# Attention kernel on one core: rows of a batch placed as 16j+f, so that a head-split tile moves in one transfer instead of four

## The chip, the cores and the metric

The kernel runs on one core of one Trainium2 chip. The metric is the device time of one execution in microseconds. Three runs of the kernel before gave 780.52, 779.7 and 776.21 us, median 779.7.

## The reference

The input x is 8 batches of 512 rows by 512 columns in float32. Each batch has a condition vector that is projected too and added to the queries and keys; 16 heads of 32 columns attend over all 512 rows, and the result is added to x.

```python
Q = _split_heads(x @ Wq.T + bq)
K = _split_heads(x @ Wk.T + bk)
V = _split_heads(x @ Wv.T + bv)
cQ = Q + _split_heads(tokens @ Wq.T + bq)
cK = K + _split_heads(tokens @ Wk.T + bk)
scores = jnp.einsum('bhqd,bhkd->bhqk', cQ, cK) / jnp.sqrt(jnp.float32(HEAD_DIM))
attn = jax.nn.softmax(scores, axis=-1)
out = jnp.einsum('bhqk,bhkd->bhqd', attn, V)
return x + out.transpose(0, 2, 1, 3).reshape(B, S, D_MODEL)
```

Nothing in it depends on the order of the 512 rows, as long as the same order is used for queries, keys, values, residual and output of a batch.

## The kernel before, in words

The work is cut into 32 items t = 4b + g: batch b, and a group g of four heads, that is 128 columns. Weights and inputs stand transposed in SBUF (features on the partitions); the projections are made by a scheme with seven products of half-size blocks instead of eight (`product`, L459, `item`). For each item the scores are computed by rows (L642), their maxima are taken on VectorE (L615), and exponentials with row sums on ScalarE (L690).

Three of the four row blocks of an item's exponentials are not computed again in transposed form but "kept": VectorE turns 32x32 blocks in place (`turn_kept`, L661), and then two block rows have to change places between partitions. That is `swap_kept` (L678): block 0 goes to a side buffer (move 0), block 1 to the place of block 0 (move 1), the side buffer to the place of block 1 (move 2). Each move is two transfers within SBUF, for the first two row blocks (part 0, 256 KB each, 32 partitions of 8 KB) and for the third (part 1, 128 KB each). Each move waits until the move ahead has landed. For the last row block the scores are computed again in transposed form (L772, L782); its exponentials (L792) and the kept ones are multiplied with V (L820, L837). L837 also reads a copy of V with its partition halves exchanged, which `cross_v` (L813) makes once per batch in two halves of two transfers.

All of these transfers stand in one queue, that of SP (SyncE), in the order in which the code is written: SP issues one after the other, and where one has to wait for data or for a landing, all behind it wait too. `step(t)` is a round of the loop. In a round SP issues: part 0's moves 0 and 1, a small transposing transfer of maxima (`turn_max`, L725), part 0's move 2, part 1's move 0, the output of item t-1 (`put`, L908), in the first round of each batch half of `cross_v`, part 1's moves 1 and 2, a chunk of the next batch's x (`load_block`, L167), the residual of item t+1 (`load_residual`, L185), and in the second round of a batch the other half of `cross_v`. L837 of item t-1, in round t, needs all moves of round t-1.

A chunk of x, a residual and an output have the same form: a tile of 128 partitions with 16 x 32 values each. Partition 32h+j, place f holds the 32 columns of head h of the group in row 32f+j of the batch. DRAM holds the rows of 512 columns, so such a tile is 2048 pieces of 32 values, 128 bytes each. In one access pattern over DRAM, partition 32h+j would be stepped by two strides (h by 32 values, j by a row), and f by a third (32 rows). The kernel issues one transfer for each h, whose pattern is `spread(a, d)`, j outermost (32), then f (16), then 32 values.

Item 30's output is made at the end in one tile and stored by `store_30` (L1377), two of the four transfers by SP and two by ACT; item 31's output is untransposed by TensorE and stored by two transfers (L1416). The first batch's x is loaded by `load_x` (L152) in four chunks of 128 rows of 2 KB.

Of the kernel before, what the change touches and what calls it, by code (L numbers as in the profile page):

```python
# [17 lines left out]
def kernel(  # L18
# [38 lines left out]
    nc = tc.nc  # L57
    P = 128
    B, S, D = x.shape
    HD = 32  # L60
    H = D // HD
    G = D // P
    HG = P // HD
    NP = HG // 2
    NS = S // P
# [66 lines left out]
    def take(n):  # L132
        got = [order.pop(0) for _ in range(n)]
        return got

    def give(*bs):
        order.extend(bs)
# [8 lines left out]
    xs = {}  # L146

    def load_x(n, queue=nc.sync):

        if n < B * NS:  # L150
            xs[n] = early[:, 3 + n, :]
            queue.dma_start(xs[n], x[n // NS, n % NS * P : (n % NS + 1) * P, :])  # L152

    BL = 32
    NB = S // BL

    def spread(a, d):

        return a.rearrange("(f j) d -> j f d", j=BL)[:, :, d : d + BL]

    def load_block(n):

        b, cc = divmod(n, NC)
        if b < B:
            xs[n] = xp.tile([P, NB, BL], F32, tag="x", name=f"x_{n}")
            for h in range(HG):
                nc.sync.dma_start(xs[n][h * BL : (h + 1) * BL], spread(x[b], cc * P + h * BL))  # L167

    xr = {}
    late = []  # L170

    def turned_by_vector(t):

        return t < T - 1

    def load_residual(t):

        b, g = divmod(t, G)
        if turned_by_vector(t):
            if t == T - 2:  # L180
                xr[t] = late[0][:, 2, :].rearrange("p (f e) -> p f e", e=BL)
            else:
                xr[t] = op.tile([P, NB, BL], F32, tag="xr", name=f"xr_{t}")
            for h in range(HG):
                nc.sync.dma_start(  # L185
                    xr[t][h * BL : (h + 1) * BL], spread(x[b], g * P + h * BL)
                )
        else:

            xr[t] = xT[b][:, g, :]  # L190
# [187 lines left out]
    def combine_x(b, half, on=nc.vector):  # L378

        if b >= B:  # L380
            return
        blk = [[xT[b][:, i * 2 : i * 2 + 2, j * HS : (j + 1) * HS] for j in range(2)] for i in range(2)]
        to = [xc[:, i, :, :] for i in range(4)]
        if half == 0:
            on.tensor_tensor(to[2], blk[1][1], blk[0][1], ALU.subtract)
            on.tensor_tensor(to[1], to[2], blk[0][0], ALU.add)
        else:
            on.tensor_tensor(to[0], blk[0][1], blk[0][0], ALU.subtract)
            on.tensor_tensor(to[3], blk[1][0], to[1], ALU.subtract)
# [240 lines left out]
    def rows(t, qc, bs):  # L630

        open_max(t)
        for j in range(HG):
            row_scores(t, qc, j, psum[:, bs[j], :])
# [30 lines left out]
    def swap_kept(t, move, part):  # L665

        qs = slice(0, 2) if part == 0 else slice(2, KQ)
        w = (qs.stop - qs.start) * HG * HS
        for h in range(2):

            def block(a):
                e = kept[t][h * 64 + a * BL : h * 64 + (a + 1) * BL, 1 - a, qs]
                return e.rearrange("p q j x e -> p (q j x e)")

            at = (1 - h) * 64 + part * BL
            side = between[at : at + BL, :w]
            to, of = [(side, block(0)), (block(0), block(1)), (block(1), side)][move]
            nc.sync.dma_start(to, of)  # L678
# [178 lines left out]
    def masked(t):  # L857

        if t in aparts:
            return aparts.pop(t)  # L860
        apart = op.tile([P, HG, NS, NS], F32, tag="apart", name=f"apart_{t}")
        nc.gpsimd.tensor_tensor(  # L862
            apart,
            sums[t].rearrange("p c h o -> p h c o").broadcast_to([P, HG, NS, NS]),
            which.unsqueeze(1).unsqueeze(1).broadcast_to([P, HG, NS, NS]),
            ALU.mult,
        )
        return apart
# [11 lines left out]
    def reciprocals(t, pd):  # L880
        rec = op.tile([P, NB, 1], F32, tag="recs", name=f"recs_{t}")
        nc.vector.reciprocal(rec, psum[:, pd, :NB].unsqueeze(2))
        return rec
# [20 lines left out]

    def put(t, y):
        b, g = divmod(t, G)
        for h in range(HG):
            nc.sync.dma_start(spread(out[b], g * P + h * BL), y[h * BL : (h + 1) * BL])  # L908

    def untranspose(o, pt):  # L910
        for qc in range(NS):
# [201 lines left out]
    def third(t):  # L1113

        if t % G == 1 and t > 1:
            cross_v(t // G, 1)
        k3 = take(HG)
        rows(t, 2, k3)
        maxima(t, 2, k3)
        row_exponentials(t, 2, k3)  # L1120
        give(*k3)
        turn_kept(t, 1)
        swap_kept(t, 0, 0)
        swap_kept(t, 1, 0)

    def rest_and_sums(t):

        hi, pd = take(1)[0], take(1)[0]
        if t in KEPT:
            times_v_rest(t, hi)  # L1130
        else:
            for kc in range(NS):
                times_v(t, kc, psum[:, hi, :])
        spread_sums(masked(t), psum[:, pd, :])
        return hi, pd
# [5 lines left out]
    def step(t):  # L1141

        b, r = divmod(t, G)
        third(t)
        at = take(2)
        multiply, leave, sums_of = item(*next(made), at)
        multiply()
        hi, pd = rest_and_sums(t - 1)
        leave(0)
        leave(1)  # L1150
        rec = reciprocals(t - 1, pd)
        give(*at, pd)
        aparts[t] = masked(t)
        sums_of()
        if r == 0:
            combine_x(b + 1, 0, nc.gpsimd)

        n = take(HG)
        rows(t + 1, KQ, n)
        maxima(t + 1, KQ, n)  # L1160
        row_exponentials(t + 1, KQ, n)
        split_max(t + 1)
        turn_max(t + 1)
        if t - 1 in KEPT:
            lo = take(1)
            y = kept_leaves(t - 1, lo[0], hi)
        else:
            lo = []
            y = turned(t - 1, hi)
        give(*n[:3], *lo, hi, n[3])  # L1170
        swap_kept(t, 2, 0)
        finish(t - 1, y, rec)
        turn_kept(t, 2)
        if t == 1:
            turn_next()
        swap_kept(t, 0, 1)
        put(t - 1, y)
        if r == 0:
            cross_v(b, 0)

        s = take(HG)
        scores_of_rest(t, s)
        rest_leaves(s)
        give(*s)
        k1 = take(HG)
        rows(t + 1, 0, k1)
        maxima(t + 1, 0, k1)
        swap_kept(t, 1, 1)
        swap_kept(t, 2, 1)
        if t > 1:  # L1190
            bias_residual(t)
        at = take(2)
        multiply, leave, sums_of = item(*next(made), at)
        multiply()
        row_exponentials(t + 1, 0, k1, (0, 1))
        leave(0)
        row_exponentials(t + 1, 0, k1, (2, 3))
        leave(1)
        give(k1[0], k1[1], at[0], k1[2], k1[3], at[1])
        turn_next()  # L1200
        if r == 0:
            combine_x(b + 1, 1, nc.gpsimd)
        sums_of()

        k2 = take(HG)
        rows(t + 1, 1, k2)
        maxima(t + 1, 1, k2)
        row_exponentials(t + 1, 1, k2)
        give(*k2)
        turn_kept(t + 1, 0)  # L1210
        more = next(made, None)
        if more:
            at = take(2)
            multiply, leave, sums_of = item(*more, at)
            multiply()
            leave(0)
            leave(1)
            sums_of()
            give(*at)
        load_blocks()  # L1220
        load_residual(t + 1)

    for t in KEPT[:-1]:
        step(t)
# [51 lines left out]
    t = T - 3  # L1276
# [12 lines left out]
    n = more_maxima(t + 1, 0)  # L1289
    lo = take(1)[0]  # L1290
    y = kept_leaves(t - 1, lo, hi)
# [25 lines left out]
    y = kept_leaves(t, lo, hi)  # L1317
# [3 lines left out]
    n = more_maxima(t + 2, 0)  # L1321
# [6 lines left out]
    t = T - 2  # L1328
# [19 lines left out]
    t = T - 1  # L1348
# [19 lines left out]
    y30 = op.tile([P, NB, BL], F32, tag="res", name=f"res_{t - 1}")  # L1368
# [4 lines left out]

    def store_30(queue, hs):
        b, g = divmod(t - 1, G)
        for h in hs:
            queue.dma_start(spread(out[b], g * P + h * BL), y30[h * BL : (h + 1) * BL])  # L1377

    store_30(nc.sync, (0, 1))
    exponentials(t, 3, (4, 2, 0, 1))  # L1380
# [13 lines left out]
    y = late[0][:, 1, :].rearrange("p (c s) -> p c s", c=NS)  # L1394
    rec = op.tile([P, NS, HG, 1], F32, tag="rec", name="rec")
    pi, po = bank(6), [bank(4), bank(2)]
    b, g = divmod(t, G)
# [10 lines left out]
    for i in range(2):  # L1408
        cs = slice(i * 2, i * 2 + 2)
        nc.vector.tensor_tensor(  # L1410
            y[:, cs].rearrange("p c (h e) -> p c h e", h=HG),
            po[i][:, two[i]].rearrange("p (c h e) -> p c h e", c=2, h=HG),
            rec[:, cs].broadcast_to([P, 2, HG, HD]),
            ALU.mult,
        )
        (nc.scalar, nc.sync)[i].dma_start(  # L1416
            out[b].rearrange("(c p) d -> p c d", p=P)[:, cs, g * P : (g + 1) * P], y[:, cs]
        )


# [29 lines left out]
```

## Time and profile before

| | |
|---|---|
| median of three runs | 779.7 us (776.21 to 780.52) |
| the profiled execution | 782.4 us, of which the span on the core is 780.6 us |
| busy, share of the span | PE 88%, DVE 76%, ACT 65%, POOL 54% |
| granted clock of TensorE | 0.931 |
| DMA packets | 233595, of them 216554 under 512 B |

The profile lists a busy time for each engine, but SP appears in it only as a queue: its rows (SPq) are the times in which a transfer was being issued, waits included. A transfer's own time is told in two ways: the share of time in which the sixteen DMA engines moved packets, and the time from issue to landing. How much of the work of a queue matters is seen from the waits of the computing engines.

### The profile page before, as it was taken

Reading aid. Unit: us, or ns where it says so; the run is one execution under the profiler, and the core shown is the slowest. Engines: PE = TensorE matmul, PEld = TensorE weight load, DVE = VectorE, ACT = ScalarE, POOL = GpSimd, SP = SyncE. Lnnn points to the kernel's source line nnn. Section 1 sums busy time; section 2 is a strip of 40 time slices with the busy share of each in tenths; the row PEclk is TensorE's granted clock in tenths of the full one; section 3 lists DMA queues with packets and bytes.
Section 4 is the critical chain, followed back from the end, with each engine's and each line's share of the span. In section 5 each row is a group of like instructions: output and inputs, shape, how many; then the busy total and the mean of one; then the engine's idle time right before and its main releaser. Section 6 shows DMA issues by size and latency. Waiting matters only on the chain. (4 is left out here: it accounts for less than half of the span.)

```text
span 780.6 us, 29911 instructions
## 1 busy us (share of the span) xinstructions
PE 688.8 (88%) x12524; PEld 397.8 (51%) x12524; DVE 592.5 (76%) x913; ACT 510.8 (65%) x1310; POOL 418.3 (54%) x537
## 2 busy tenths in 40 slices
PE   9999989859989599896998769988799979997697
PEld 7444545535546355453555345554455546554352
DVE  3895997738896398883988839968498858888567
ACT  2584887638885287863877828858388848885145
POOL 2716474835657256673566716657266755653230
PEclk9999999979999799996999969989799979998789
DMA  6444677767666776776666677767767766767711
GB/s 172 76 72 96 132 156 155 152 150 139 142 144 143 155 146 137 154 163 150 136 136 143 158 159 145 152 138 148 166 136 151 157 151 141 151 140 161 170 25 28
DMA packets 233595, 107.86 MB, mean 138 GB/s; under 512 B 216554, under 2 KB 217066, under 8 KB 227892
## 3 DMA queue, kind: packets, MB, share of 16 engines
q1 hardware_dynamic: 231700, 104.90, 64.4%
q8 instruction: 98, 1.61, 0.9%
q10 hardware_dynamic: 1760, 1.05, 0.5%
q14 instruction: 37, 0.30, 0.1%
HBM read 19.75 MB, written 8.39 MB: 36 GB/s over the span
## 5 line engine op out<-in xcount | busy, mean ns | idle before, releaser
L615 DVE TENSOR_REDUCE nmax<-psum 128x1 f32<-128x512 f32 x498 | 305.5, 674 | 32.9 <-PE psum L642 32.7
L690 ACT ACTIVATE store<-psum,nmax 128x512 f32<-128x512 f32 x348 | 235.7, 692 | 41.1 <-DVE nmax L615 40.6
L661 DVE STREAM_TRANSPOSE store<-store 128x1024 f32<-128x1024 f32 x174 | 204.2, 1212 | 0.0
L642 PE MATMUL psum<-kT,qT 32*128 32x512 f32 x1024 | 164.9, 645 | 2.0 <-ACT store L690 1.5
L792 ACT ACTIVATE store<-psum 128x512 f32<-128x512 f32 x116 | 59.9, 604 | 137.6 <-PE psum L782 137.6
L837 PE MATMUL psum<-store,v 64*32 64x192 f32 x1856 | 69.0, 397 | 57.1 <-DMA store<-store 39.8
L894 DVE STREAM_TRANSPOSE res<-psum 128x192 f32<-128x192 f32 x58 | 18.9, 363 | 130.1 <-issue 111.5
L690 ACT ACTIVATE psum<-psum,nmax 128x512 f32<-128x512 f32 x132 | 87.1, 660 | 32.3 <-DVE nmax L615 31.6
L902 POOL TENSOR_TENSOR res<-res,recs 128x512 f32<-128x512 f32 x30 | 31.4, 1047 | 123.5 <-DVE res L895 120.9
L837 PEld LDWEIGHTS psum<-store,v 64*32 64x32 f32 x1856 | 44.5, 126 | 91.0 <-issue 39.8
L837 PE MATMUL psum<-store 64*32 64x192 f32 x1856 | 67.3, 388 | 24.3 <-DMA store<-v 23.4
L642 PEld LDWEIGHTS psum<-kT,qT 32*128 32x128 f32 x1024 | 54.7, 191 | 37.6 <-ACT store L690 19.5
L690 ACT ACTIVATION_READ_ACCUMULATOR store<-psum,nmax 128x1 f32 x348 | 72.9, 210 | 0.0
L837 PEld LDWEIGHTS psum<-store 64*32 64x32 f32 x1856 | 50.1, 127 | 31.5 <-DMA store<-v 27.2
L459 PE MATMUL psum<-wc_v,xc 128*32 128x256 f32 x768 | 47.7, 379 | 0.1
L198 POOL TENSOR_TENSOR xr<-xr,bvs 128x512 f32<-128x512 f32 x30 | 38.5, 1285 | 12.0 <-DMA x<-in_x_dram 8.5
L459 PE MATMUL psum<-xc,wc_q 128*32 128x256 f32 x720 | 44.5, 379 | 0.0
L459 PE MATMUL psum<-xc,wc_k 128*32 128x256 f32 x720 | 44.5, 379 | 0.0
L782 PEld LDWEIGHTS psum<-qT,kT 32*128 32x128 f32 x928 | 38.2, 220 | 4.3 <-issue 3.3
L903 POOL TENSOR_TENSOR res<-res,xr 128x512 f32<-128x512 f32 x30 | 38.5, 1284 | 2.4
L782 PE MATMUL psum<-qT,kT 32*128 32x128 f32 x928 | 38.4, 307 | 0.9 <-issue 0.8
L862 POOL TENSOR_TENSOR apart<-sums,which 128x64 f32<-128x64 f32 x30 | 8.8, 292 | 53.9 <-ACT store L690 53.9
(207 smaller groups left out, 1109.9 us busy)
## 6 DMA issues: line engine op xcount, KB each, us to landing
store<-store SPq DMA_DIRECT2D x174, 256.0 KB, 3.4
store<-store SPq DMA_DIRECT2D x174, 128.0 KB, 3.0
store<-v SPq DMA_DIRECT2D x32, 256.0 KB, 3.8
out_dram<-res SPq DMA_DIRECT2D x122, 64.0 KB, 2.8
xr<-in_x_dram SPq DMA_DIRECT2D x120, 64.0 KB, 2.8
x<-in_x_dram SPq DMA_DIRECT2D x112, 64.0 KB, 2.5
w_q<-in_L_cond_Wq_dram SPq DMA_DIRECT2D x4, 256.0 KB, 3.8
w_v<-in_L_cond_Wv_dram SPq DMA_DIRECT2D x16, 64.0 KB, 2.4
```

Source lines behind the costliest of these rows:

```text
L198: nc.gpsimd.tensor_tensor(xr[t], xr[t], bias, ALU.add)
L459: nc.tensor.matmul(pt[r], still[:, r], moving, start=(kc == kcs[0]), stop=(kc == kcs[-1]))
L615: nc.vector.tensor_reduce(nmax[t][:, qc, j : j + 1, 0], pt, AX.X, ALU.max, negate=True)
L642: nc.tensor.matmul(pt, qkT["q", t][r, qc * P : (qc + 1) * P], qkT["k", t][r, :], start=True, stop=True,)
L661: nc.vector.transpose(e, e)
L690: nc.scalar.activation(to, of, AF.Exp, bias=nmax[t][:, qc, j, :], accum_out=sums[t][:, qc, j, :],)
L782: nc.tensor.matmul(psum[:, bs[j], kc * P : (kc + 1) * P], qkT["k", t][r, kc * P : (kc + 1) * P], qkT["q", t][r, R:], start=False, stop=(kc ...
L792: nc.scalar.activation(rest_of[:, j], psum[:, bs[j], :], AF.Exp)
L837: nc.tensor.matmul(psum[j * HD : (j + 1) * HD, (lo, hi)[h], : R // 2], v[half, c, (g * HG + j) * HD : (g * HG + j + 1) * HD], kept[t][half ...
L894: nc.vector.transpose(to[:, h], of.rearrange("p (c s) -> p c s", c=KQ))
L902: nc.gpsimd.tensor_tensor(y, y, rec.broadcast_to([P, NB, BL]), ALU.mult)
L903: nc.gpsimd.tensor_tensor(y, y, xr.pop(t), ALU.add)
```

## The change

Position 32f+j of a batch now holds row 16j+f instead of row 32f+j. With that, j and f step through the rows of a batch in one piece (row 16j+f), and the DRAM side of a whole tile can be written as one pattern with three steps: h outermost (4 steps of 32 values), then the 512 rows, then 32 values. A chunk of x, a residual and an output each become one transfer of 256 KB. `blocks(a, c)` is that pattern.

The other places follow: `load_x` reads rows 16j+f for four values of f at a time (DRAM pattern: f outermost with 4, then j with 32, then 512 values). `store_30` stores two heads by one transfer of 128 KB. The last item's output goes out by four transfers of 64 KB instead of two of 128 KB, two from each queue. And one line of `step` is moved: part 0's move 2 stands behind part 1's move 0, instead of ahead of it. The condition, biases and weights are loaded as before.

```diff
-            queue.dma_start(xs[n], x[n // NS, n % NS * P : (n % NS + 1) * P, :])
+            at = n % NS * HG
+            queue.dma_start(xs[n], x[n // NS].rearrange("(j f) d -> f j d", f=S // HD)[at : at + HG])
...
+    def blocks(a, c):
+
+        return a.rearrange("(j f) (c h e) -> c h j f e", f=NB, h=HG, e=BL)[c]
...
-            for h in range(HG):
-                nc.sync.dma_start(xs[n][h * BL : (h + 1) * BL], spread(x[b], cc * P + h * BL))
+            nc.sync.dma_start(xs[n].rearrange("p f e -> p (f e)"), blocks(x[b], cc))
...
-            for h in range(HG):
-                nc.sync.dma_start(
-                    xr[t][h * BL : (h + 1) * BL], spread(x[b], g * P + h * BL)
-                )
+            nc.sync.dma_start(xr[t].rearrange("p f e -> p (f e)"), blocks(x[b], g))
...
-        for h in range(HG):
-            nc.sync.dma_start(spread(out[b], g * P + h * BL), y[h * BL : (h + 1) * BL])
+        nc.sync.dma_start(blocks(out[b], g), y.rearrange("p f e -> p (f e)"))
...
-        swap_kept(t, 2, 0)
         finish(t - 1, y, rec)
         turn_kept(t, 2)
         if t == 1:
             turn_next()
         swap_kept(t, 0, 1)
+        swap_kept(t, 2, 0)
         put(t - 1, y)
...
-        for h in hs:
-            queue.dma_start(spread(out[b], g * P + h * BL), y30[h * BL : (h + 1) * BL])
+        of = y30[hs[0] * BL : (hs[-1] + 1) * BL].rearrange("p f e -> p (f e)")
+        queue.dma_start(blocks(out[b], g)[hs[0] : hs[-1] + 1], of)
...
-        (nc.scalar, nc.sync)[i].dma_start(
-            out[b].rearrange("(c p) d -> p c d", p=P)[:, cs, g * P : (g + 1) * P], y[:, cs]
-        )
+        rows_of = out[b].rearrange("(j c a) d -> c a j d", c=NS, a=HG)
+        for c in (i * 2, i * 2 + 1):
+            (nc.scalar, nc.sync)[i].dma_start(rows_of[c][:, :, g * P : (g + 1) * P], y[:, c])
```

Where this stands in SP's queue: first, before the change, the two loads at the end of round 2 and the first rows of round 3 (x is the chunk, xr the residual, maxT the transposed maxima, store the exponentials, res the output; behind the names stands the shape that is written, and "x4" counts equal rows).

```order
L167 DMA x_1376<-in_x_dram 32x16x32 x4
L185 DMA xr_1381<-in_x_dram 32x16x32 x4
L678 DMA store<-store 32x2048 x4
L725 DMA_TRANSPOSE maxT_1480<-split 128x1x128
L678 DMA store<-store 32x2048 x2
L678 DMA store<-store 32x1024 x2
L908 DMA out_dram<-res_1546 32x16x32 x4
L678 DMA store<-store 32x1024 x4
```

The same place after the change (line numbers are up to four higher).

```order
L171 DMA x_1337<-in_x_dram 128x16x32
L188 DMA xr_1339<-in_x_dram 128x16x32
L679 DMA store<-store 32x2048 x4
L726 DMA_TRANSPOSE maxT_1435<-split 128x1x128
L679 DMA store<-store 32x1024 x2
L679 DMA store<-store 32x2048 x2
L908 DMA out_dram<-res_1501 4x512x32
L679 DMA store<-store 32x1024 x4
```

The two kinds of moves that follow the transposing transfer have changed places, and each x, xr and output counts one row instead of four. An output is written in the shape 4x512x32: four heads outermost. For the two loads the same pattern stands on the side that is read.

The second place is the end of SP's queue, before the change: the outputs of items 29 (the last `put`), 30 and 31.

```order
L908 DMA out_dram<-res_9666 32x16x32 x4
L1377 DMA out_dram<-res_9858 32x16x32 x2
L1416 DMA out_dram<-store 128x2x128
```

And after the change.

```order
L908 DMA out_dram<-res_9402 4x512x32
L1377 DMA out_dram<-res_9591 2x512x32
L1418 DMA out_dram<-store 4x32x128 x2
```

The last stores now are written with 4, 2 and 4 as outermost count; ACT's queue has the same two kinds of rows at its end. On PE, DVE, ACT and POOL no computing instruction moves.

## The prediction

> **What bounds the kernel now.** I read the waits first, then SP's timeline, then the list of transfers. Among the waits, the engine with the most work, PE, stands still mainly in front of one line (name of the waiting line, what it waited for, us in total, times, longest):
>
> ```profile
> PE psum L837 <- DMA store<-store: 39.8, 13, 6.3
> PE psum L837 <- DMA store<-v: 23.4, 7, 4.9
> ```
>
> The kept exponentials come too late from their exchange, and the copy of V from its own: 63.2 us. The stretch table (length, then busy time of PE, PEld, DVE, ACT, POOL, granted clock, share of time in which the DMA engines moved packets, GB/s) says how much PE idles in the loop at all:
>
> ```profile
> 100.00:730.00 630.00, 551.21 (x10804) 325.36 (x10804) 483.52 (x726) 430.66 (x1123) 359.17 (x462) 0.92 0.71 149
> ```
>
> 630 - 551.2 = 78.8 us. So most of PE's idling is a wait for transfers, and the queue that issues them has to be read. One round in SP's timeline (start, us, line, transfer, count; waits are inside the us):
>
> ```profile
> 288.63 6.22 SPq L678 DMA_DIRECT2D store<-store  x4
> 294.95 1.18 SPq L725 DMA_TRANSPOSE maxT<-split  x1
> 296.22 3.40 SPq L678 DMA_DIRECT2D store<-store  x4
> 299.68 3.03 SPq L908 DMA_DIRECT2D out_dram<-res  x4
> 302.81 3.65 SPq L678 DMA_DIRECT2D store<-store  x4
> 306.55 2.21 SPq L167 DMA_DIRECT2D x<-in_x_dram  x4
> 308.81 2.66 SPq L185 DMA_DIRECT2D xr<-in_x_dram  x4
> 311.57 0.51 SPq L678 DMA_DIRECT2D store<-store  x1
> ```
>
> One row begins where the last ends: SP is never free. It is the chain of issues and landings on SP that sets the round. The rounds' length comes from the first, the 22nd and the last of the rows with which a round starts:
>
> ```profile
> 74.29 4.87 SPq L678 DMA_DIRECT2D store<-store  x4
> ...
> 573.10 5.92 SPq L678 DMA_DIRECT2D store<-store  x4
> ...
> 723.70 9.92 SPq L678 DMA_DIRECT2D store<-store  x8
> ```
>
> 21 rounds with a chunk of x take 498.8 us (23.8 each), 7 without 150.6 us (21.5 each), together 649.4 us.
>
> **The pieces.** The list of transfers (count, KB each, us to landing) and the load of SP's DMA queue (packets, MB, share of sixteen engines' span):
>
> ```profile
> q1 hardware_dynamic: 231700, 104.90, 64.4%
> ...
> store<-store SPq DMA_DIRECT2D x174, 256.0 KB, 3.4
> store<-store SPq DMA_DIRECT2D x174, 128.0 KB, 3.0
> ...
> out_dram<-res SPq DMA_DIRECT2D x122, 64.0 KB, 2.8
> xr<-in_x_dram SPq DMA_DIRECT2D x120, 64.0 KB, 2.8
> x<-in_x_dram SPq DMA_DIRECT2D x112, 64.0 KB, 2.5
> ...
> store<-in_cond_dram SPq DMA_DIRECT2D x1, 16.0 KB
> store<-in_L_cond_bq_dram SPq DMA_DIRECT2D x1, 2.0 KB
> ...
> bvl<-in_L_cond_bv_dram SPq DMA_DIRECT2D x1, 0.5 KB, 2.1
> ```
>
> What does a piece of 128 bytes cost? In this stretch the queue carries only weight transfers of such pieces:
>
> ```profile
> 17.00:25.00 8.00, 8.00 (x42) 2.98 (x42) 4.09 (x10) 1.86 (x3) 2.37 (x3) 1.00 0.77 121
> ```
>
> 121 GB/s for 8 us are 7560 pieces; 0.77 of 16 engines for 8 us are 98.6 engine-us; so 13.0 ns a piece. The change leaves the pieces as they are: a tile is 2048 of them, 26.6 engine-us, before and after. Dealt to 16 engines that is 1.7 us, to 4 engines 6.7 us, to 2 (1024 pieces) 6.7 us too.
>
> **How many engines share a transfer** decides the result. Before, each pattern that matters has 32, 64 or 128 as outermost count. After, the DRAM side has h outermost, 4 (2 in the store of item 30, 4 in the first batch's load and in the last stores). No row shows such a transfer of weight; three small ones bear on it, at the start:
>
> ```profile
> 0.72 0.41 SPq L227 DMA_DIRECT2D w_q<-in_L_cond_Wq_dram  x1
> ...
> 1.66 0.38 SPq L249 DMA_DIRECT2D store<-in_cond_dram  x1
> 2.09 0.23 SPq L250 DMA_DIRECT2D store<-in_L_cond_bq_dram  x1
> 2.36 0.25 SPq L251 DMA_DIRECT2D store<-in_L_cond_bk_dram  x1
> ```
>
> 128 rows take 0.41 us to issue, 8 rows 0.38, one row 0.23 and 0.25, though a row is 2 KB in all of them; and in the list above exactly those with 8, 1 and 1 rows have no landing, while the bias of 128 values in 0.5 KB has one. Landings are paired with issues by the number of completion marks, so these three came with another number than the rest. I take it that a transfer is dealt out along its outermost dimension, over at most as many engines as that dimension has steps.
>
> The Trainium skill, "DMA: Bandwidth & Descriptors", section "Why a DMA increments its semaphore by 16 and not by 1", says so outright: the number of engines is the largest up to 16 that divides the outermost count of both sides, and the lowest-numbered engines are used. By that rule the tiles here go over four engines, always the same four; no run here shows it yet for a transfer with 4 outermost.
>
> **Part by part, with four engines.** Load first. The queue's work is 0.644 x 780.6 x 16 = 8043 engine-us. 360 transfers of 512 pieces (112 x, 124 xr, 124 out) are 2396 of it, the weights 186; the rest, 5461, is 341 us on each engine, 11.8 for each of 29 rounds. Three tiles add 20.0 us a round on the four engines: 31.8 us where they had 16.8. This alone exceeds the round: 21 x 31.8 + 7 x 25.1 = 844 us, +194.
>
> The order in the queue adds to it, since an exchange needs all sixteen engines and stands behind tiles on four of them. I walk a round from the issue of the last move (part 1's move 2) at 0:
> - The chunk and the residual are issued by 1.6 us; their pieces begin at 2.6 (a 64 KB transfer takes 2.8 us with 0.4 of pieces, so 2.4 of fixed time, of which I put 1.5 ahead) and occupy the four engines until 16.0.
> - Part 0's move 0, long issued, moves behind them, 2.3 us for two transfers (3.4 - 2.4 is about 1 each), and has landed at 19.1.
> - Move 1 waits for that: issued 19.1 and 19.6, landed after 3.4 at 23.0. The transposing transfer (1.2) and part 1's move 0 are issued meanwhile.
> - Part 0's move 2 waits for move 1: issued 23.0 to 24.1. The output is issued behind it; its pieces run from 26.5 to 33.2.
> - Part 1's move 1 is issued at 24.7, but its packets stand behind the output's: landed at 35.
> - Part 1's move 2 waits for that, at 35 the next round begins; half a copy of V per round adds 1.
>
> So 36 us, and 29.3 without x: 21 x 36 + 7 x 29.3 = 961 us, **+312**. PE waits in front of L837 some 14 us a round; its other work, and DVE's and POOL's, fits in.
>
> The saved issues (nine a round, about 0.55 us each, 4.9 us) gain nothing then: SP waits longer for landings. A 256 KB issue I cost at 0.5, between the 0.23 of one row and four times 0.55; at the upper end two of them a round delay what follows by about 2 each, 4 us. The moved line: move 2 of part 0 goes behind part 1's move 0, which waits for VectorE's turning. The rows before that turning are, on the chain of waits and among the groups (mean ns behind the busy time):
>
> ```profile
> 573.00 2.76 PE psum L837 x128
> ```
>
> ```profile
> L661 DVE STREAM_TRANSPOSE store<-store 128x1024 f32<-128x1024 f32 x174 | 204.2, 1212 | 0.0
> ```
>
> Landing 3.5, L837 about 3, two turnings of 1.2 and the output's own, some 1: done about 10 us into the walk, before SP gets there at 21. It costs nothing, and is in the walk. Its bounds are the two issues it trades, 1.1 us a round either way.
>
> Start: the chunks of the first batch, pieces of 2 KB.
>
> ```profile
> 3.00:9.00 6.00, 5.62 (x38) 5.07 (x36) 1.62 (x5) 1.78 (x4) 0.00 (x0) 1.00 1.00 358
> ```
>
> All engines are busy there, 22.4 GB/s each. 1.05 MB over four takes 11.7 us, with their share of the weights 15.3, instead of 6.4: the last chunk comes 9 us later, and PE turns it now in this row, without slack:
>
> ```profile
> 9.64 1.04 PE L356 MATMUL psum<-ident,store 128*128 128x128 f32 x8
> ```
>
> With the first chunks by blocks **+10**. Around the rounds: the first has two chunks of x (+6.7), and after 723.7 an output stands once more ahead of an exchange (6.7 - 1.7): **+12**. End:
>
> ```profile
> 775.86 0.85 SPq L1377 DMA_DIRECT2D out_dram<-res  x2
> 775.87 0.93 ACTq L1377 DMA_DIRECT2D out_dram<-res  x2
> ...
> 777.40 0.41 SPq L1416 DMA_DIRECT2D out_dram<-store  x1
> ```
>
> Now the span ends 3.2 us after the last issue. After, each half of item 30 is 1024 pieces on the same two engines, 13.3 us together, from 777.4 to 790.7; the last stores' 512-byte rows follow on four engines, some 2 us, and the landing: 794.5, **+14**.
>
> Sum: 780.6 + 312 + 10 + 12 + 14 = 1129 us of span; the execution stood at 782.4, 2.7 above the median of 779.7. **1128 us.**
>
> **Rivals.**
> 1. *All sixteen engines share the transfer* (faster; the mechanism: it is dealt out by partition or piece). Then 4.9 us of issue a round go, DMA waits of PE (63.2 us) are the gain and 78.8 its cap: about 780 - 60 = 720 us. For it: SP is never free, and the chain runs through its issues; a transfer of 256 KB lands in 3.4 us, one of 64 KB in 2.8. Against it: the three small transfers. It decides if the pieces of a tile run 16 wide; 0.14. The Trainium skill, same page, "Rules for kernel authors", advises to coalesce small transfers into a large one; the landings just named agree, and by that rule the time would be this one.
> 2. *Four engines, but the order costs nothing*: exchanges are not held up by tiles beyond the engines' load. +194 + 36 = about 1010 us. For it: a swap's packets on idle engines may run faster than now. Against: each move waits for the landing ahead. 0.16.
> 3. *Sixteen engines, but an issue costs by the piece*: 2 us for a tile, as four had; 780 us. Against: 128 rows issue in 0.41 and 512 pieces in 0.55. 0.04.
>
> **How the numbers follow.** The forecast has 0.66. Its own bounds: downward the pure load, 1010, and 980 if the exchanges run a tenth faster beside idle engines (1 of 11.8 us a round, some 30 in all); upward 4 us a round for long issues and landings that are slower: the exchanges' median is
>
> ```profile
> DMA to landing us min/median/max: 2.2/3.2/5.1
> ```
>
> and one or two more of the chain's landings at 5.1 instead of 3.2 make 2 us a round; 6 x 28 = 168 on 1128 gives 1290. 980 to 1290 holds nearly all of the forecast and of rival 2, 0.78. What a measurement of this kernel can tell from no change is 0.5%. Faster 0.14, within 0.5% 0.04, slower 0.82.
>
> **What would show it.** Right: the share of DMA engines' time falls from 0.71 to about 0.5 with the pieces unchanged; x, xr and out take 8 us or more to land, or have no landing at all, as the 8-row transfer; L837 waits about 14 us a round for store<-store; the span ends some 17 us after the last computing instruction. Wrong: landings of the tiles near 3.5 us and SP with free time in a round; then rival 1. Rounds of 32 us without long landings behind the output would be rival 2.

## The result, and the profile after

The changed kernel takes 1012.98 us (median of 4 runs, 1012.03 to 1015.0) against 780.11 us before in the same comparison: a ratio of 1.2985, 95% interval 1.2911 to 1.306. The profiled execution has a span of 1010.9 us, 230.3 more than before.

In the list of transfers after (count, KB each, us to landing where it is told) the tiles and all others have lost their landing:

```profile
q1 hardware_dynamic: 226298, 104.88, 50.9%
...
store<-store SPq DMA_DIRECT2D x174, 256.0 KB
...
xr<-in_x_dram SPq DMA_DIRECT2D x30, 256.0 KB
out_dram<-res SPq DMA_DIRECT2D x30, 256.0 KB
x<-in_x_dram SPq DMA_DIRECT2D x28, 256.0 KB
```

The bytes are the same (104.88 MB, 104.90 before). Why the landings are missing no view says. I read it, as I did for the three small transfers, as completion marks in another number, which the profile can't pair with issues. It is a weak sign: in e8 and e10 below, two stores of item 30 with an unchanged pattern have no landing either, and in e9 the exchanges keep theirs beside outputs that lost them.

The number of packets says more. The queue has 5402 fewer than before, though the pieces are the same. If each transfer adds as many packets as it has engines, the 361 transfers on this queue whose pattern the change touches (358 of tiles, two first loads, a last store) added 361 x 16 = 5776 before. After, 93 transfers with 4 as outermost count (89 of tiles, two first loads, two last stores) and one with 2 (half of item 30) add 93 x 4 + 2 = 374. The difference is 5402, to the packet.

How wide a tile moves is seen from two stretches of one round, the first within an output, the second within a chunk and a residual (length, busy time of PE, PEld, DVE, ACT, POOL, granted clock, share of time in which the DMA engines moved packets, GB/s):

```profile
267.00:271.00 4.00, 0.00 (x0) 0.00 (x0) 1.55 (x3) 2.59 (x8) 2.42 (x6) 0.96 0.40 45
277.00:284.00 7.00, 7.00 (x166) 4.53 (x154) 2.60 (x5) 1.51 (x4) 1.60 (x2) 0.72 0.35 57
```

57 GB/s, where the weights' pieces of the same size moved at 121 before. In six of the seven microseconds the rate is 54 or 55 GB/s (in the one from 281 to 282 us it is 71), so I count 54 for the tiles. If four engines do it, each starts a piece every 9.5 ns (54 GB/s / 4 / 128 bytes), and every 11.4 ns in an output.

The round in SP's timeline (start, us, line, transfer, count):

```profile
250.32 9.41 SPq L679 DMA_DIRECT2D store<-store  x4
259.84 1.19 SPq L726 DMA_TRANSPOSE maxT<-split  x1
261.13 2.45 SPq L679 DMA_DIRECT2D store<-store  x4
263.62 0.62 SPq L908 DMA_DIRECT2D out_dram<-res  x1
264.29 9.96 SPq L679 DMA_DIRECT2D store<-store  x4
274.30 0.61 SPq L171 DMA_DIRECT2D x<-in_x_dram  x1
274.96 4.72 SPq L188 DMA_DIRECT2D xr<-in_x_dram  x1
```

An output is issued in 0.62 us, where four took 3.03, but the two moves behind it take 9.96 instead of 3.65: move 1 of part 1 stands behind the output's pieces, and move 2 waits for its landing. The first moves of a round take 9.41 instead of 6.22, behind the chunk and the residual, and the residual's own issue lasts 4.72 us. In the rounds without a chunk a residual is issued in 0.62 us, so it seems that SP can't put it into the queue faster than the chunk leaves it.

Who pays is seen in the waits:

```profile
PE psum L838 <- DMA store<-store: 194.0, 26, 13.7
POOL xr L199 <- DMA xr<-in_x_dram: 68.4, 18, 14.1
PE psum L838 <- DMA store<-v: 50.2, 7, 8.9
```

PE's waits for exchanges went from 39.8 to 194.0 us, for the copy of V from 23.4 to 50.2. Most of the rest is PE's own busy time, 722.9 us after 688.8, at a granted clock of 0.836 instead of 0.931. In the stretch of 277 to 284 us above, right after such a wait, the clock is 0.72.

The rounds, from the first, the 22nd and the last start:

```profile
91.70 4.95 SPq L679 DMA_DIRECT2D store<-store  x4
...
748.07 9.00 SPq L679 DMA_DIRECT2D store<-store  x4
...
938.34 10.66 SPq L679 DMA_DIRECT2D store<-store  x8
```

21 rounds with x take 656.4 us (31.3 each, 23.8 before), 7 without 190.3 (27.2, 21.5 before). So 17.4 us of the 230.3 lie ahead of the rounds (91.70 against 74.29), 197.2 in them, and 15.7 behind (72.6 us against 56.9).

### The profile page after: what moved, and what is told of

The parts are those of the page before. It is cut to its first block, busy times and chain, and to the rows that moved or that the text cites. A ratio compares the mean times of both kernels' runs of the same rounds, so it can differ in the third digit from the quotient of the medians.

```text
span 1010.9 us, 29422 instructions
## 1 busy us (share of the span) xinstructions
PE 722.9 (72%) x12524; PEld 415.2 (41%) x12524; DVE 592.1 (59%) x913; ACT 510.8 (51%) x1310; POOL 417.5 (41%) x537
## 3 DMA queue, kind: packets, MB, share of 16 engines
q1 hardware_dynamic: 226298, 104.88, 50.9%
## 5 line engine op out<-in xcount | busy, mean ns | idle before, releaser
L838 PE MATMUL psum<-store,v 64*32 64x192 f32 x1856 | 90.0, 485 | 203.0 <-DMA store<-store 194.0
L838 PEld LDWEIGHTS psum<-store,v 64*32 64x32 f32 x1856 | 53.3, 151 | 245.8 <-issue 208.6
L838 PE MATMUL psum<-store 64*32 64x192 f32 x1856 | 79.4, 429 | 50.2 <-DMA store<-v 50.2
L691 ACT ACTIVATE psum<-psum,nmax 128x512 f32<-128x512 f32 x132 | 87.0, 659 | 32.3 <-DVE nmax L616 31.5
L838 PEld LDWEIGHTS psum<-store 64*32 64x32 f32 x1856 | 58.9, 146 | 61.8 <-DMA store<-v 54.1
L460 PE MATMUL psum<-xT,wT_k 128*32 128x256 f32 x480 | 35.6, 393 | 0.0
```

What stands on the lines that cost most here:

```text
L460: nc.tensor.matmul(pt[r], still[:, r], moving, start=(kc == kcs[0]), stop=(kc == kcs[-1]))
L691: nc.scalar.activation(to, of, AF.Exp, bias=nmax[t][:, qc, j, :], accum_out=sums[t][:, qc, j, :],)
L838: nc.tensor.matmul(psum[j * HD : (j + 1) * HD, (lo, hi)[h], : R // 2], v[half, c, (g * HG + j) * HD : (g * HG + j + 1) * HD], kept[t][half ...
```

## Experiments

My theory: a transfer is dealt out over as many DMA engines as its outermost dimension allows, here four; and since all stand in one queue, the exchanges are held up behind the tiles. Its rivals: the size of a transfer is what costs; the new order of rows is slow in DRAM; only the load of the four engines counts, not the order; the moved line has a part.

**e1: one transfer for a tile, but wide.** From the kernel before:

```diff
+    def wide(a, c):
+        return a.rearrange("(p r) (k c e) -> c p r k e", p=P, c=HG, e=BL)[c]
...
-            for h in range(HG):
-                nc.sync.dma_start(xs[n][h * BL : (h + 1) * BL], spread(x[b], cc * P + h * BL))
+            nc.sync.dma_start(xs[n].rearrange("p (r k) e -> p r k e", r=NS), wide(x[b], cc))
```

and the same for residuals and outputs.

> The kernel before, with its order of rows, but each chunk, residual and output (but the last batch's outputs) as one transfer of 256 KB whose outermost count is 128: partition p takes four rows of one DRAM pattern, sixteen pieces of 128 bytes. The pieces and bytes are as before, but other rows and columns are read and written, so the values are not the reference's. If the outermost count decides how many engines share a transfer: the tiles run sixteen wide, SP saves nine issues a round, and the time is below that of before, about 720 us. If a transfer of 256 KB itself is what holds up the exchanges: near the changed kernel's 1013 us. If an issue costs by the piece: 780 us.

Measured: 749.81 us, ratio 0.9632 (0.9567 to 0.9696). In the built kernel the DRAM side becomes one step of 2048 pieces, the SBUF side keeps 128 outermost. The list of transfers has landings again, and the queue's packets say sixteen engines: 4176 fewer than before (231700) for 261 fewer transfers, 16 for each.

```profile
q1 hardware_dynamic: 227524, 104.88, 67.7%
...
xr<-in_x_dram SPq DMA_DIRECT2D x30, 256.0 KB, 4.7
x<-in_x_dram SPq DMA_DIRECT2D x28, 256.0 KB, 3.6
out_dram<-res SPq DMA_DIRECT2D x28, 256.0 KB, 4.7
```

So size falls as a cause: the same bytes in as few transfers make the kernel faster. Half of the 60 us that I gave this case came; PE's waits for exchanges fell from 39.8 to 22.5 us, not to nothing: SP still waited 191.8 us for landings of the moves.

**e2: the new order of rows, four transfers a tile.** From the changed kernel (moved line put back, first loads and last stores by heads as well):

```diff
-            nc.sync.dma_start(xs[n].rearrange("p f e -> p (f e)"), blocks(x[b], cc))
+            for h in range(0, HG, 1):
+                nc.sync.dma_start(xs[n][h * BL : (h + 1) * BL].rearrange("p f e -> p (f e)"), blocks(x[b], cc)[h : h + 1])
```

> The changed kernel's order of rows (16j+f), but each tile again in four transfers, one for each head, whose outermost count is 512 in DRAM and 32 in SBUF; the moved line is put back. If the number of engines is the cause: as before, 780 us within 1%. If reading and writing rows in the new order is itself slow in DRAM: clearly above, over 850 us.

Measured: 811.65 us, 1.0389 (1.0342 to 1.0437). Neither: most of the 30% is gone, 4% stays. It isn't DRAM: the landings are those of before.

```profile
out_dram<-res SPq DMA_DIRECT2D x122, 64.0 KB, 2.6
xr<-in_x_dram SPq DMA_DIRECT2D x120, 64.0 KB, 2.8
x<-in_x_dram SPq DMA_DIRECT2D x112, 64.0 KB, 2.5
```

But a residual's issue takes longer on SP, 627 ns (median of 120) instead of 488, first before, then in e2 (count, shortest, median and longest issue in ns):

```profile
L185 SPq DMA_DIRECT2D xr<-in_x_dram x120: 321/488/1944, 49.5 to 720.8; - x120
L192 SPq DMA_DIRECT2D xr<-in_x_dram x120: 575/627/1896, 53.5 to 748.6; - x120
```

Twelve issues a round at about 0.13 us more are 1.6 us, 44 in 28 rounds; the rounds grew by 24.4. The size would do, but no run shows that this makes the 4%: PE's wait for exchanges did not grow (37.3 us), while POOL's for residuals did, from 3.4 to 18.7 us. What makes the issue longer was not tried by itself. In e1, e2 and the changed kernel the DRAM side of these transfers is merged into steps of another shape than the SBUF side, and they issue in about 0.62 where nothing ahead holds them up; the first loads of e2, in the new order but with 32 x 512 on both sides, in 0.3 to 0.46. So the shape is the likely cause rather than the order of rows; neither was changed alone.

**e3: two transfers a tile, two heads outermost.** From the changed kernel, the loop of e2 with a step of 2, `[h : h + 2]`.

> The changed kernel with two transfers of 128 KB for each tile, two heads outermost. If the outermost count is the number of engines: two engines instead of four, the three tiles of a round take 30 us of each of the two instead of 15, so 21 x 15 + 7 x 10 = 385 us more, about 1400 us. If the size of a transfer is what costs: between before and after, about 900 us.

Measured: 1445.39 us, in a single run. Halving the size made it 43% slower than the changed kernel. Two stretches in which a chunk and a residual move:

```profile
438.00:442.00 4.00, 4.00 (x101) 2.40 (x86) 3.35 (x6) 2.07 (x4) 2.33 (x2) 1.00 0.19 31
442.00:446.00 4.00, 4.00 (x68) 1.89 (x64) 3.38 (x7) 3.64 (x10) 0.00 (x0) 1.00 0.19 31
```

31 GB/s with 2 outermost, 57 with 4. Both contain a short burst of something else: without it (440 to 442 and 444 to 446 us here) the rates are 27 and 54, that is 13.5 GB/s for each step in both. The queue's packets are as many as in the changed kernel (226298), as they must be if twice as many transfers add half as many each. In e9 below they are 1800 fewer than in e2 (230044 after 231844): 30 outputs, each with 4 packets instead of 4 x 16. Rates and packets together settle the first half of the theory.

**e4: chunks and residuals from ACT's queue.** From the changed kernel, `nc.sync` to `nc.scalar` in `load_block` and `load_residual`.

> The changed kernel with chunks and residuals issued by ACT, so that they stand in another queue than the exchanges, on the same four engines. If the order in the queue costs, as in my walk: the first exchange of a round no longer stands behind two tiles; rounds of about 27 us instead of 31, 900 us. If only the load of the four engines counts: unchanged, about 1010 us.

Measured: 1011.77 us, 1.2968 (1.2888 to 1.3047), as the load rival said. But it proves little, because a new wait came in:

```profile
PE psum L643 <- ACT store L691: 135.4, 22, 14.0
ACT store L691 <- DMA store<-store: 120.8, 14, 11.3
```

The second row names an exchange, but in ACT's timeline (start, us; in brackets the idle time before) such a wait lies inside the issue of a residual:

```profile
249.76 8.54 ACTq L188 DMA_DIRECT2D xr<-in_x_dram  x1
...
258.48 0.69 ACT L691 ACTIVATE store<-psum,nmax 128x512 f32<-128x512 f32 x1 [7.57 <-DMA store<-store]
```

ACT now stands still while its issues wait for room (8.5 us for a residual), and PE waits for ACT instead of for the exchanges (57.5 us left of 194.0). The question of order stays open here; e9 takes it up.

**e5 and e6: the moved line.** e5 is the kernel before with the line moved, e6 the changed kernel with the line put back:

```diff
-        swap_kept(t, 2, 0)
         finish(t - 1, y, rec)
...
         swap_kept(t, 0, 1)
+        swap_kept(t, 2, 0)
         put(t - 1, y)
```

> The kernel before with the moved line alone (part 0's move 2 behind part 1's move 0). If SP's waits for landings are part of the round: SP issues two transfers while move 1 is on its way instead of waiting, up to 1 us a round, so 755 to 780 us. If the wait only changes its place: 780 us within 0.5%.

> The changed kernel without the moved line. If the four engines are the bound: 1013 us within 1%, since what SP saves is waited for in front of the engines. If the line helps there as well: up to 1 us a round more, 1040 us.

e5: 782.21 us, 1.002 (0.9993 to 1.0047). e6: 1010.39 us, 1.2932 (1.2882 to 1.2981), which overlaps the changed kernel's interval. The line does nothing to be measured in either. SP's waits, and then its rows, show where the microsecond goes:

```profile
SPq L678 <- DMA store<-store: 131.4, 83, 3.7
SPq L1377 <- POOL res L1372: 22.8, 1, 22.8
SPq L678 <- DVE store L661: 11.0, 8, 5.9
```

In e5 SP waits 24 us less for landings than before (155.7), 5 us more for VectorE (11.0 instead of 6.2), and the round is no shorter. Most of the rest is in the issue of the outputs, which now follows the moves at once: added up over the loop (74 to 725 us), SP's rows of moves became 22 us shorter (378 to 356) and its rows of outputs 20 us longer (71 to 91).

**e9: the output alone in one transfer.** e2, with `put` as in the changed kernel.

> As the kernel of e2 (new order of rows, four transfers for a tile, old place of the moved line), but the output alone goes in one transfer of 256 KB with four heads outermost. If only the load of the four engines counts: they have 11.8 + 2 x 1.7 + 5.8 = 21 us of work a round, less than the 24 us that a round takes, so no loss, and three issues a round less: 812 us or below. If the place in the queue counts (part 1's move 1 stands behind the output's pieces, and SP waits for its landing): 5.8 - 1.5 = 4.4 us a round more, less 1.9 of issues, 28 rounds: about 880 us.

Measured: 893.75 us, 1.1481 (1.1355 to 1.1607). The engines had room, and still the kernel lost 82 us on e2. SP's timeline shows the place:

```profile
333.06 2.86 SPq L683 DMA_DIRECT2D store<-store  x4
335.97 0.65 SPq L912 DMA_DIRECT2D out_dram<-res  x1
338.04 7.91 SPq L683 DMA_DIRECT2D store<-store  x4
346.05 2.62 SPq L174 DMA_DIRECT2D x<-in_x_dram  x4
```

The moves behind the output take 7.91 us (3.4 to 4.9 in e2), and PE's wait for exchanges is 120.0 us (37.3 in e2). The rounds grew by 80.5 us on e2, 2.9 each; by the walk 2.5. So the order in the queue costs, and the rival of pure load falls. How the changed kernel's loss divides between outputs and loads was not measured.

**e7, e8, e10, e11: SP relieved without touching the patterns.** From the kernel before: e7 issues chunks and residuals from ACT, e8 the outputs from POOL, e10 outputs and chunks from POOL, e11 all three from POOL:

```diff
-            nc.sync.dma_start(spread(out[b], g * P + h * BL), y[h * BL : (h + 1) * BL])
+            nc.gpsimd.dma_start(spread(out[b], g * P + h * BL), y[h * BL : (h + 1) * BL])
```

> The kernel before with chunks and residuals (still four transfers for a tile) issued by ACT instead of SP. If the issues on SP's queue are what makes the exchanges late: SP saves eight issues a round, PE's 63 us of waits for transfers shrink, about 745 us. If an issue costs ACT as much as it costs SP and ACT's own chain counts: 780 us or more.

> The kernel before with the outputs issued by POOL, which computes them, instead of SP. If the issues on SP's queue are what makes the exchanges late: four issues a round less and no wait of SP for POOL, about 760 us. If making descriptors for pieces of 128 bytes costs POOL more than it has free (9 us a round): above 780 us.

> The kernel before with outputs and chunks of x issued by POOL. If SP's issues are what makes the exchanges late, as e8 says: another four issues a round less on SP, about 760 us. If POOL's 2.6 us for four issues come in the way of its sums: above the 770 us of e8.

> The kernel before with outputs, chunks and residuals issued by POOL: SP is left with the exchanges, maxima and copies of V. POOL has 7.8 us of issues a round beside 14.4 us of sums, so it is busy for nearly all of a round: if POOL's issues are hidden, about 750 us; if POOL becomes the bound, above 780 us.

Measured: e7 836.77 us, 1.0736 (1.0682 to 1.079): ACT's chain can't bear the issues. Its exponentials stand 83.1 us in front of what the profile names as residuals, which they don't read; in the timeline such a wait, 4.54 us, covers the 3.92 us in which ACT issued one. e8 769.96, 0.9855 (0.98 to 0.9909), two runs. e10 **742.85 us, 0.954 (0.9444 to 0.9637)**, faster than both kernels. e11 754.14, 0.9694 (0.9528 to 0.986), two runs, with POOL busy for 86% of the span. In e10 the waits are:

```profile
PE psum L837 <- DMA store<-v: 27.7, 7, 5.8
...
PE psum L837 <- DMA store<-store: 13.9, 11, 5.7
```

The exchanges' part fell from 39.8 to 13.9 us: the gain that fewer issues on SP had to give is there, and about as large as with e1. It can be had without narrowing the transfers.

## Why the prediction was right, and where it wasn't

**The direction and the mechanism held.** That the outermost count deals a transfer out was read from three small transfers' issue times and missing landings; the missing landings turned out to be a weak sign, but the rates and the packets of the changed kernel (4), e3 (2) and e1 (128 in SBUF, 2048 in DRAM) bear the rule out. The Trainium skill, "DMA: Bandwidth & Descriptors", section "Why a DMA increments its semaphore by 16 and not by 1", gives the largest divisor of both outermost counts up to 16 as the number of engines; the trace agrees, with 54 GB/s at 4 and 27 at 2. That the lowest-numbered engines are taken no view here shows.

**The size was off: 1128 forecast, 1012.98 measured.** The range held it; the sum did not.

| term | forecast | measured in the spans |
|---|---|---|
| ahead of the rounds | +10 | +17.4 |
| in the rounds | +312, and 6.7 for the first | +197.2 |
| behind them | +5 and +14 | +15.7 |

The term that was mis-sized is the piece: "so 13.0 ns a piece". It came from a stretch in which SP's issues, not the engines, set the pace (sixteen issues of 64 KB one after the other in 8.43 us are 124 GB/s, and 121 moved), and from the busy share, which adds up how long packets last. On four engines the share was 0.35 of sixteen, that is 5.6 engines' time on four: packets overlap. What counts is how often one starts, every 9.5 ns in loads and 11.4 in outputs. A tile then takes 4.9 or 5.8 us instead of 6.7, and the same walk gives 36 - 2 x 1.8 - 0.9 = 31.5 us a round with x, 26.6 without: 31.3 and 27.2 were measured. These sizes come from the trace after, so this shows that the walk fits, not that it could have been forecast.

The start was under-counted: PE turned the last two chunks 8.4 us later (at 18.00 instead of 9.64), near the 9 us of the forecast, but the first tiles by blocks, at 4.7 us of issue each, also held up the first copies of V and POOL's sums; for one of these PE waited 6.1 us.

Of the signs named beforehand, most came: no landings, a DMA share of 0.55 in the loop (100 to 930 us), a span that ends 16 us after the last computing instruction. One did not: L838 (L837 before) waited 194.0 us for exchanges in 28 rounds, 6.9 us a round and not 14. The rounds with x were 4.7 us shorter than forecast, and PE, at the lower clock that the forecast left out, was itself busy some 1.2 us longer in each.

**Rival 2 named 1010 us, and is still wrong.** "Four engines, but the order costs nothing" used the same 13.0 ns. The piece too long and the order left out happened to cancel, so its number was luck. With the measured pieces it would be at most 27.4 us a round, 22.5 without x, 733 us of rounds where 846.6 were measured. e9 shows the order's cost alone.

**The saved issues gained nothing**, as forecast: SP had 9 fewer a round, and its rows for moves and residuals grew by more than that. **The moved line** cost nothing, as forecast (e5, e6). **Rival 1** did not happen, but e1 and e10 show its worth: 4 to 5%, not the 60 us that I gave as nearly all of PE's waits. The Trainium skill, same page, "Rules for kernel authors", advises to coalesce small transfers; e1 agrees, but only as the pattern stayed wide.

**Not foreseen:** the 0.13 us longer issue in e2, which may be its 4%. In the changed kernel, where SP waits anyway, it probably doesn't show.

What stays open is why such an issue is longer, and how much of e4's unchanged time is load and how much ACT's standing still.

## What to carry to other kernels

Before several transfers are joined into one, look at the outermost count of the joined pattern on both sides: here 32 and 128 ran wide, 4 moved at 54 GB/s and 2 at 27, and what stood behind such a transfer in the queue waited. A queue that carries urgent transfers in a chain is relieved by moving the patient ones to an engine with free time, as POOL here (and not ACT, e7), not by making them fewer and narrower. To price a piece, take GB/s from a stretch in which the DMA engines are the bound; the busy share says how long packets last, not how often they start.

## What the runs showed that I had not expected

- An issue can block: with a 256 KB tile on four engines ahead of it, the next tile's issue took SP 4.72 us (median of 30 residuals 4.716), and ACT 8.5 us in e4.
- Packets of one DMA engine overlap: 13 ns by the busy share, one every 9.5 ns in loads.
- POOL issues a 64 KB tile part in 0.65 us (2.60 for four), about as long as SP takes in e2, and such outputs land in 3.9 us in e10.
